# Two neighbouring chunks per block transpose of Q and K, the odd chunks moved to their partitions by transfers

## The chip, the core and the metric

One core of one Trainium2 chip runs the whole program. The metric is the device time of one execution in microseconds (us). Before the change three runs took 794.63, 798.83 and 799.25 us, so the median is 798.83 us. The profiled execution of the same kernel took 792.66 us, of which 790.9 us lie between its first and its last instruction (its span); 1.8 us lie around it.

## What is computed

Sixteen sequences of 256 tokens with 256 features go through four blocks, each added to its input and normalised: a Fourier mixing layer with a cumulative sum, a layer of eight gated low-rank experts, softmax attention with 16 heads of 16 features, and a feed-forward layer with ternary weights. The change touches only the attention:

```python
qkv = jnp.einsum('bld,ed->ble', x, W_qkv)
qkv = qkv.reshape(b, 3, H, L, D_H)              # H = 16, L = 256, D_H = 16
Q, K, V = (qkv[:, 0], qkv[:, 1], qkv[:, 2])
scores = jnp.einsum('bhqd,bhkd->bhqk', Q, K) * D_H ** (-0.5)
attn = jax.nn.softmax(scores, axis=-1)
out = jnp.einsum('bhqk,bhkd->bhqd', attn, V)
out = out.transpose(0, 2, 1, 3).reshape(b, L, D_IN)
return jnp.einsum('bld,ed->ble', out, W_o)
```

Two things in it matter here. The reshape doesn't split the features into heads: the 256 x 768 numbers of one sequence are read on as one row, cut into chunks of 16, and 256 chunks in a row are one head of Q, K or V. One token holds 48 chunks (`NJ`), so a head takes the chunks of 5 1/3 tokens. And softmax does not care in which order the keys are summed, so long as keys and values agree, nor does a row of the result depend on where its query stands.

## The kernel before

**Groups and stages.** The sequences go in four groups of four (`GB = 4`). `attention(i)` handles group i: a projection stage, a first pass over the scores for the row maxima, a second pass for exp and the product with V, and the output projection. `front(b)` computes the first two blocks of a sequence, `back(b)` the feed-forward block. While `attention(i)` runs, the fronts of group i+1 and the backs of group i-1 are worked in between. The projection stage of a group begins only after the last score of the group before it has been read, because it writes over the same tile `zt`; so the four attentions stand one behind the other.

**Projection and transposes.** The 256 tokens of each sequence are cut into 8 blocks `tb` of 32 tokens. For each block TensorE makes a tile of 128 partitions (4 sequences x 32 tokens) by 768 in two PSUM banks (L831, 64 instructions in a group: 32 chunks in one bank, 16 in the other). For the six blocks that hold Q and K VectorE transposes blocks of 32 x 32 from PSUM into `zt` (L840). A chunk has 16 features and the block wants 32, so each chunk is read twice: partitions 32g to 32g+15 of `zt` hold the features of sequence g, partitions 32g+16 to 32g+31 a second copy that nothing uses, except that partition 32g+16 is overwritten later. Blocks 5 to 7 (part of K, and V) are also copied to SBUF (`evacuate`) and sent to HBM (`vd`, L849), from where V is read back with one key in each partition (L868).

**The extra row.** Partition 32g+16 is a seventeenth feature: ones for the keys (L858), and for the queries the negative row maximum (L914). With it, one matmul gives score minus maximum. In the first pass (L894) the scores of one head are taken for all four sequences (16 instructions), VectorE reduces each bank to row maxima (L903, four for a head), and after four heads TensorE transposes the maxima (L907), ScalarE copies them to `nmT` (L908) and transfers put them into their rows of `zt` (L914). The second pass (L933) reads them; then follow exp on ScalarE (L942), the product with V (L948), a transpose back by VectorE (L956) and the division by the sum.

**Queues.** Every transfer is issued from SyncE's queue (SP), in one order. The transfers go round eight semaphores, and each waits until the transfer eight places before it has landed.

**The order of work.** The kernel records its operations first. A planner (`Order.run`) then takes, at each step, the operation that could start earliest by its own table of durations, ties broken by `order.prio`, and pins that order on every engine. Each engine's order is therefore fixed before the run, whatever the true durations are. The order of heads is 14, 15, 0, 1, 2, 3, 4, 5, 12, 13, 6 ... 11, that of the blocks 5, 2, 0, 3, 6, 7, 1, 4.

The places that the prediction names:

| line before | what |
|---|---|
| L831, L840 | projection matmuls; block transposes into `zt` |
| L849, L868 | V out to HBM; V back |
| L858, L914 | row of ones for the keys; negative maxima for the queries |
| L894, L903 | first-pass scores; their maxima |
| L933, L942, L948, L956 | second-pass scores; exp; product with V; transpose back |
| L977, L981, L991 | attention output: transposes, their copy into `oT`, output projection |
| L1027, L1056 | feed-forward matmuls of a back |

Of the kernel before, what the change touches and what calls it, by code (L numbers as in the profile page):

```python
# [18 lines left out]
P = 128  # L19
D = 256  # L20
S = 256
# [264 lines left out]
def forward(ctx, tc, x, xt, wq, wkv, wo0T, f0, degen, cs, wqkvT, wo1T, wfc, wproj, cst, out):  # L286
# [23 lines left out]
    ztv = zt_.rearrange("p (l j) -> p j l", j=NJ)  # L310
# [508 lines left out]
    def attention(i):  # L819
# [4 lines left out]
        for n, tb in enumerate((5, 2, 0, 3, 6, 7, 1, 4)):  # L824
            order.prio = base - 60.0 + n
            for j0, nj in ((0, 32), (32, 16)):
# [10 lines left out]
                if tb < ZT:  # L837
                    dve(
                        [(z[tb], j0)], [b], nj * 32,
                        lambda b=b, tb=tb, j0=j0, nj=nj: V.transpose(  # L840
                            ztv[:, j0 : j0 + nj, ts(tb, 32)], b.v.unsqueeze(2).to_broadcast([P, nj, 2, HD])
                        ),
                        us=nj * 32 * 1.72e-3,
                    )
                if tb >= VT // 32:
# [7 lines left out]
                    )  # L853

            heads = [h for h in range(H) if k_at(h) == tb]
            for g in range(GB if heads else 0):
                op(
                    (SP, 0.1, lambda g=g, lo=ZQ + heads[0] * S, n=len(heads) * 2: nc.sync.dma_start(  # L858
                        zt_[32 * g + HD : 32 * g + HD + 1, lo : lo + n * P].rearrange("o (c q) -> o c q", q=P),
                        a(ones)[0:1, :].unsqueeze(1).to_broadcast([1, n, P]),  # L860
                    )),
                    [(rowk[tb], g)], [ones, z[tb]],
                )
        order.prio = base - 20.0
        for half, lo, n, at in ((0, 28, 4, 12), (0, 0, 12, 0), (1, 12, 16, 0)):
            for g in range(GB):
                op(
                    (SP, 0.5, lambda g=g, half=half, lo=lo, n=n, at=at: nc.sync.dma_start(  # L868
                        va[half][:, at : at + n, g, 0:HD],
                        vd.slot.ap[g].rearrange("t e -> (t e)")[(2 * ZQ + lo * P) * HD - VT * NJ * HD :][: n * P * HD].rearrange("(n p d) -> p n d", p=P, d=HD),  # L870
                    )),
                    [(v[half], (g, at))], [vd],
                )

        def part(g, rows, which, h, at=0, n=S):
            lo = which * ZQ + h * S + at
            return zt_[32 * g : 32 * g + rows, lo : lo + n]
# [7 lines left out]
        for q in range(4):  # L885
            nm, nmT, heads = tile_("nm", [P, GB, 4, 2]), tile_("nmT", [32, P]), HEADS[4 * q : 4 * q + 4]
            for k, h in enumerate(heads):
                order.prio = base + 6.0 * (4 * q + k - 8)
                sc = [ps([P, 2, S], "a") for _ in range(GB)]

                def go(sc=sc, h=h):
                    for t in range(2):
                        for g in range(GB):
                            T.matmul(  # L894
                                sc[g].v[:, t, :], part(g, HD, 0, h, t * P, P), part(g, HD, 1, h),
# [4 lines left out]
                for g in range(GB):  # L900
                    dve(
                        [(nm, (k, g))], [sc[g]], 512,
                        lambda nm=nm, sc=sc, g=g, k=k: V.tensor_reduce(nm.v[:, g, k, :], sc[g].v, AX.X, ALU.max, negate=True),  # L903
# [3 lines left out]
            pe([b], [nm, small], 0.11, lambda b=b, nm=nm: T.transpose(b.v, nm.v.rearrange("p g h t -> p (g h t)"), ident))  # L907
            act([nmT], [b], 128, lambda b=b, nmT=nmT: A.copy(nmT.v, b.v))  # L908
            runs = [heads] if heads[3] - heads[0] == 3 else [heads[0:2], heads[2:4]]
            for g in range(GB):  # L910
                for r, run in enumerate(runs):
                    n = len(run) * 2
                    op(
                        (SP, 0.1, lambda g=g, lo=run[0] * S, n=n, at=8 * g + r * n, nmT=nmT: nc.sync.dma_start(  # L914
                            zt_[32 * g + HD : 32 * g + HD + 1, lo : lo + n * P].rearrange("o (c q) -> o c q", q=P),
                            nmT.v[at : at + n, :],
                        )),
                        [(rowq[q], (g, r))], [nmT, *{q_at(h): z[q_at(h)] for h in run}.values()],
                    )

        for hp in range(H // 2):
            av = ps([P, 2, S], "a")
            for hk in range(2):
                n = hp * 2 + hk
                h = HEADS[n]
                order.prio = base + 6.0 * n
# [227 lines left out]
```

## Time and profile before

Engine time in the profiled execution (792.66 us, span 790.9 us, mean granted TensorE clock 0.921):

| engine | busy us | share of the span |
|---|---|---|
| TensorE matmuls (PE) | 744.1 | 94% |
| TensorE weight loads (PEld, beside PE) | 527.2 | 67% |
| VectorE (DVE) | 642.3 | 81% |
| ScalarE (ACT) | 476.6 | 60% |
| GpSimd (POOL) | 124.0 | 16% |

The four projection stages start at 100.05, 238.45, 421.46 and 589.85 us, and the first second-pass score of each group (L933) at 152.59, 291.43, 477.20 and 642.43 us. Before 100 us the fronts of the first group run, after 722 us only the backs of the last one.

Transfers issued from SP for the attention, in the whole program:

| line | what | count | KB each |
|---|---|---|---|
| L849 | V out | 24 | 256 or 128 |
| L858 | ones | 64 | 2 or 6 |
| L868 | V back | 48 | 32, 96 or 128 |
| L914 | maxima | 96 | 2 or 4 |

A row of groups reads: line, engine, operation, output from input, shapes, count; after the bar busy us and mean ns of one; after the second bar the idle time of the engine just ahead, and who ended it. In the timeline a row merges neighbouring instructions of one line: start, us, engine, line, operation, names, count, and in brackets the idle time ahead. "PE busy" counts a matmul until its modelled end, so that a TensorE that waits in small steps or runs at a lower clock still looks busy. SP's transfers are listed with the time the queue spends on issuing.

### The profile page before, as it was taken

What the parts mean: (1) busy time and instruction counts of PE and PEld (TensorE: products, weight loads), DVE (VectorE), ACT (ScalarE), POOL (GpSimd) and SP (SyncE); (2) the same over time, 40 slices, a digit from 0 to 9 for tenths busy, and PEclk for the clock granted to TensorE, in tenths of its full rate; (3) what the DMA queues carried; (4) which work ended last, traced back from release to release, by engine and by line L of the source; (5) the groups of instructions that cost most, each with busy time, mean ns of one, the idle gap of its engine ahead of it and who ended that gap; (6) DMA issues with size and microseconds to landing.
All of it is one profiled execution on the core that took longest, in us unless ns stands there. A gap on an engine that the chain in (4) does not pass through costs nothing.

```text
span 790.9 us, 15263 instructions
## 1 busy us (share of the span) xinstructions
PE 744.1 (94%) x5664; PEld 527.2 (67%) x5664; DVE 642.3 (81%) x1513; ACT 476.6 (60%) x942; POOL 124.0 (16%) x306
## 2 busy tenths in 40 slices
PE   9999499999999999999999999999989999999794
PEld 6786256665566667777676767765566787766784
DVE  1999989888987997998789999897567978756554
ACT  5865531238782238988765644966721297875973
POOL 1022000101110020222122012021020002011123
PEclk9999699679999988999999989997989699999986
DMA  8101015200001450001011350000001700000000
GB/s 292 40 27 41 13 24 79 57 15 16 29 15 25 67 69 2 16 27 30 2 40 49 60 38 16 15 16 2 15 1 35 76 10 16 14 16 15 1 28 27
DMA packets 87662, 27.18 MB, mean 34 GB/s; under 512 B 68700, under 2 KB 84900, under 8 KB 87588
## 3 DMA queue, kind: packets, MB, share of 16 engines
q1 hardware_dynamic: 87588, 26.21, 15.7%
q8 instruction: 45, 0.74, 0.4%
q14 instruction: 29, 0.24, 0.1%
HBM read 16.76 MB, written 8.91 MB: 32 GB/s over the span
## 4 chain that ended last, share of the span: by engine, by line
PE 68%; DVE 18%; ACT 9%; issue 3%; POOL 2%; DVEq 0%; ACTq 0%; POOLq 0%
PE bank L831 10%; PE bank L894 9%; PE bank L948 8%; PE bank L933 8%; PE bank L1056 7%; PE bank L609 5%; DVE nm L903 5%; PE bank L1027 5%; PE bank L991 3%; PE bank L708 3%; PE bank L793 2%; PE bank L732 2%; DVE st L569 2%; ACT zt L942 1%; ACT hi L1044 1%
## 5 line engine op out<-in xcount | busy, mean ns | idle before, releaser
L942 ACT ACTIVATE zt<-bank 128x512 f32<-128x512 f32 x256 | 133.4, 596 | 57.2 <-PE bank L933 52.3
L903 DVE TENSOR_REDUCE nm<-bank 128x2 f32<-128x512 f32 x256 | 158.8, 679 | 11.1 <-PE bank L894 10.2
L563 POOL TENSOR_SCALAR st<-st 128x2 f32<-128x2 f32 x80 | 23.4, 293 | 535.6 <-DVE st L571 369.7
L894 PE MATMUL bank<-zt 16*128 16x256 f32 x1024 | 100.4, 445 | 2.2 <-DVE nm L903 1.7
L894 PEld LDWEIGHTS bank<-zt 16*128 16x128 f32 x1024 | 63.7, 205 | 29.9 <-DVE nm L903 8.7
L831 PE MATMUL bank<-wqr,x2T 128*128 128x512 f32 (+1 forms) x256 | 83.2, 486 | 0.0
L933 PE MATMUL bank<-zt 17*128 17x256 f32 x1024 | 82.5, 415 | 0.3 <-DVE nm L903 0.3
L948 PE MATMUL bank<-zt,v 128*32 128x256 f32 x1024 | 78.6, 412 | 0.0
L1027 PE MATMUL bank<-xs,w1T 128*128 128x256 f32 x512 | 75.3, 299 | 0.5 <-DVE xs L1017 0.4
L1056 PE MATMUL bank<-w2T,hi 128*128 128x256 f32 x256 | 72.1, 312 | 3.5 <-ACT hi L1044 2.5
L1056 PE MATMUL bank<-w2T,lo 128*128 128x256 f32 x256 | 69.1, 302 | 6.0 <-DVE lo L1046 6.0
L1027 PEld LDWEIGHTS bank<-xs,w1T 128*128 128x128 f32 x512 | 67.6, 199 | 9.2 <-issue 3.7
L840 DVE STREAM_TRANSPOSE zt<-bank 128x1024 f32<-128x1024 f32 (+1 forms) x48 | 64.2, 1456 | 11.3 <-PE bank L831 5.0
L831 PEld LDWEIGHTS bank<-wqr,x2T 128*128 128x128 f32 x256 | 48.5, 190 | 34.2 <-issue 28.5
L933 PEld LDWEIGHTS bank<-zt 17*128 17x128 f32 x1024 | 51.8, 191 | 22.5 <-issue 12.4
L609 PE MATMUL bank<-wf,x 128*128 128x512 f32 x128 | 62.8, 623 | 0.0
L1056 PEld LDWEIGHTS bank<-w2T,hi 128*128 128x128 f32 x256 | 52.8, 206 | 14.1 <-issue 9.1
L564 POOL TENSOR_TENSOR st<-st,mhalf 128x2 f32<-128x2 f32 x80 | 59.4, 743 | 6.8 <-POOL st L563 0.2
L1056 PEld LDWEIGHTS bank<-w2T,lo 128*128 128x128 f32 x256 | 52.7, 206 | 7.5 <-DVE lo L1046 7.5
L1046 DVE TENSOR_TENSOR lo<-work,hi 128x512 fp32r<-128x512 f32 x64 | 42.7, 681 | 15.9 <-ACT hi L1044 15.8
L948 PEld LDWEIGHTS bank<-zt,v 128*32 128x32 f32 x1024 | 29.7, 114 | 35.1 <-issue 14.8
L1036 ACT ACTIVATE work<-bank 128x512 f32<-128x512 f32 x64 | 37.8, 591 | 20.4 <-PE bank L1027 16.2
(196 smaller groups left out, 1260.2 us busy)
## 6 DMA issues: line engine op xcount, KB each, us to landing
x<-in_xT SPq DMA_DIRECT2D x16, 256.0 KB
out<-work SPq DMA_DIRECT2D x16, 256.0 KB
x<-in_x SPq DMA_DIRECT2D x12, 256.0 KB
vd<-work SPq DMA_DIRECT2D x12, 256.0 KB
v<-vd SPq DMA_DIRECT2D x16, 128.0 KB
vd<-work SPq DMA_DIRECT2D x12, 128.0 KB
v<-vd SPq DMA_DIRECT2D x16, 96.0 KB
oT<-in_wfc SPq DMA_DIRECT2D x4, 256.0 KB
```

Of the source, the lines that this page charges most:

```text
L564: pool([dst], [dst, mhalf], 0.7, lambda: G.tensor_tensor(dst.v, dst.v, a(mhalf)[:, 0:n], ALU.pow))
L609: T.matmul(pb.v.rearrange("p a s k -> p (a s k)"), xT.v[:, c, ts(t, P)], a(wf)[:, c].rearrange("p a s f -> p (a s f)"), start=(c == 0), st ...
L831: T.matmul(b.v.rearrange("p j d -> p (j d)"), x2T.v[:, c, tb].rearrange("p g k -> p (g k)"), a(wqr)[:, c, j0 * HD : (j0 + nj) * HD], start ...
L840: lambda b=b, tb=tb, j0=j0, nj=nj: V.transpose(ztv[:, j0 : j0 + nj, ts(tb, 32)], b.v.unsqueeze(2).to_broadcast([P, nj, 2, HD])),
L894: T.matmul(sc[g].v[:, t, :], part(g, HD, 0, h, t * P, P), part(g, HD, 1, h), start=True, stop=True,)
L903: lambda nm=nm, sc=sc, g=g, k=k: V.tensor_reduce(nm.v[:, g, k, :], sc[g].v, AX.X, ALU.max, negate=True),
L933: T.matmul(sc[g].v[:, c, :], part(g, HD + 1, 1, h, c * P, P), part(g, HD + 1, 0, h), start=True, stop=True,)
L942: act([e], [sc[g]], 512, lambda e=e, sc=sc, g=g: A.activation(e.v, sc[g].v, AF.Exp, scale=HD ** -0.5))
L948: T.matmul(av.v[32 * g : 32 * g + 32, hk, :], v_part(g, h, c), es[g].v[:, c, :], start=(c == 0), stop=(c == 1),)
L1027: T.matmul(pb.v[:, i, :], a(w1T)[:, n // 2, ts(q * 2 + i, P)], xs.v[:, n % 2, n // 2, :], start=(n == 0), stop=(n == 3),)
L1046: dve([(lo, q)], [h, (hi, q)], 512, lambda h=h, part=part: V.tensor_tensor(part(lo), h.v, part(hi).bitcast(F32), ALU.subtract), us=0.63)
L1056: T.matmul(pw.v[:, t, :], part.v[:, k, ts(t, P)], a(w2T)[:, k, :], start=(k + n == 0), stop=(k + n == HID // P),)
```

## The change

The 32 x 32 block is now filled by two neighbouring chunks instead of one chunk twice. A transpose thus reads each chunk once and writes half as many elements: even chunks land in partitions 32g to 32g+15 as before, odd chunks in 32g+16 to 32g+31. The odd ones must lie in the first 16 partitions for the matmul, so for each block and sequence a transfer moves them there, into a second half of `zt` that starts at column `ODD` = 4608. Queries and keys of a head now stand in two halves, 128 even and 128 odd; the same holds for the maxima and for V, which is read back in two transfers, even and odd keys. On the way out, the copy into `oT` puts even and odd queries back in turn. The rows of ones and of maxima are written once for each half, so their transfers double in number and halve in size. The matmuls keep their count and sizes; a moving operand is now two stretches of 128 columns. The planner gets a shorter duration for the transpose; the rewritten priorities have the same values as before.

```diff
-    ztv = zt_.rearrange("p (l j) -> p j l", j=NJ)
+    ODD = ZT * 32 * NJ // 2
+    ztv = zt_[:, 0:ODD].rearrange("p (l j) -> p j l", j=NJ // 2)
+    zt2 = zt_[:, 0 : 2 * ODD].rearrange("p (t c) -> p t c", t=2)
...
                     dve(
-                        [(z[tb], j0)], [b], nj * 32,
+                        [(z[tb], j0)], [b], nj * HD,
                         lambda b=b, tb=tb, j0=j0, nj=nj: V.transpose(
-                            ztv[:, j0 : j0 + nj, ts(tb, 32)], b.v.unsqueeze(2).to_broadcast([P, nj, 2, HD])
+                            ztv[:, j0 // 2 : (j0 + nj) // 2, ts(tb, 32)],
+                            b.v.rearrange("p (j t) d -> p j (t d)", t=2),
                         ),
-                        us=nj * 32 * 1.72e-3,
+                        us=nj * HD * 1.43e-3,
                     )
...
+            if tb < ZT:
+                width = 32 * NJ // 2
+                for g in range(GB):
+                    op(
+                        (SP, 0.1, lambda g=g, lo=tb * width: nc.sync.dma_start(
+                            zt_[32 * g : 32 * g + HD, ODD + lo : ODD + lo + width],
+                            zt_[32 * g + HD : 32 * g + 2 * HD, lo : lo + width],
+                        )),
+                        [(z[tb], ("odd", g))], [(z[tb], 0), (z[tb], 32)],
+                    )
...
             for g in range(GB if heads else 0):
-                op(
-                    (SP, 0.1, lambda g=g, lo=ZQ + heads[0] * S, n=len(heads) * 2: nc.sync.dma_start(
+                for t in range(2):
+                    op(
+                        (SP, 0.1, lambda g=g, lo=t * ODD + (H + heads[0]) * P, n=len(heads): nc.sync.dma_start(
...
-                        [(rowk[tb], g)], [ones, z[tb]],
+                        [(rowk[tb], (g, t))], [ones, z[tb]],
...
-                    (SP, 0.5, lambda g=g, half=half, lo=lo, n=n, at=at: nc.sync.dma_start(
-                        va[half][:, at : at + n, g, 0:HD],
+                for t in range(2):
+                        (SP, 0.3, lambda g=g, t=t, half=half, lo=lo, n=n, at=at: nc.sync.dma_start(
+                            va[half][:, at + t : at + n : 2, g, 0:HD],
...
-        def part(g, rows, which, h, at=0, n=S):
-            lo = which * ZQ + h * S + at
-            return zt_[32 * g : 32 * g + rows, lo : lo + n]
+        def some(g, rows, which, h, t):
+            lo = t * ODD + (which * H + h) * P
+            return zt_[32 * g : 32 * g + rows, lo : lo + P]
+        def every(g, rows, which, h):
+            lo = (which * H + h) * P
+            return zt2[32 * g : 32 * g + rows, :, lo : lo + P]
...
-                                sc[g].v[:, t, :], part(g, HD, 0, h, t * P, P), part(g, HD, 1, h),
+                                sc[g].v[:, t, :].rearrange("p (t q) -> p t q", t=2), some(g, HD, 0, h, t), every(g, HD, 1, h),
...
-                        (SP, 0.1, lambda g=g, lo=run[0] * S, n=n, at=8 * g + r * n, nmT=nmT: nc.sync.dma_start(
+                    for t in range(2):
+                            (SP, 0.1, lambda g=g, t=t, lo=t * ODD + run[0] * P, n=len(run), at=8 * g + 4 * t + r * 2, nmT=nmT: nc.sync.dma_start(
...
-        oT = tile_("oT", [P, 2, GB, S // 32, 32])
+        oT = tile_("oT", [P, 2, GB, P, 2])
...
-                    lambda c=c, half=half: oT.v[:, c, :, half * 4 : half * 4 + 4, :].rearrange("p g u k -> p u g k"),
+                    lambda c=c, half=half: oT.v[:, c, :, :, half].rearrange("p g (u k) -> p u g k", k=32),
```

## The prediction

> **What bounds the kernel now.** I read the page first: how busy the engines are, and which engines the chain of work that ended last runs through.
>
> ```profile
> PE 744.1 (94%) x5664; PEld 527.2 (67%) x5664; DVE 642.3 (81%) x1513; ACT 476.6 (60%) x942; POOL 124.0 (16%) x306
> PE 68%; DVE 18%; ACT 9%; issue 3%; POOL 2%; DVEq 0%; ACTq 0%; POOLq 0%
> ```
>
> TensorE leads, VectorE comes second, so halving a VectorE operation could pay. Where it pays depends on the stage, so next I cut the first two attentions at the start of the projection, at its end and at the first second-pass score. Columns: busy us of PE, PEld, DVE, ACT, POOL, then clock, DMA share, GB/s.
>
> ```profile
> 100.00:120.80 20.80, 20.80 (x68) 11.99 (x66) 17.77 (x20) 7.03 (x12) 0.00 (x0) 1.00 0.12 29
> 120.80:152.60 31.80, 31.37 (x218) 23.43 (x219) 29.33 (x56) 5.82 (x14) 1.71 (x5) 0.79 0.49 72
> 152.60:238.40 85.80, 83.08 (x774) 50.63 (x768) 74.96 (x210) 59.18 (x128) 12.16 (x35) 0.92 0.06 20
> 238.40:259.20 20.80, 20.80 (x66) 12.05 (x65) 16.38 (x17) 3.45 (x9) 0.00 (x0) 1.00 0.12 29
> 259.20:291.40 32.20, 32.20 (x247) 20.97 (x246) 31.25 (x68) 8.40 (x17) 3.73 (x11) 0.99 0.55 79
> 291.40:421.50 130.10, 129.62 (x1140) 95.86 (x1140) 114.22 (x307) 106.26 (x209) 30.54 (x80) 0.95 0.07 20
> ```
>
> Three stages, three limits. The projection is PE's: its 64 matmuls stand in the chain as one piece of 20.6 us without a gap. From there to the first second-pass score VectorE is nearly full (29.3 of 31.8 us), with the maxima L903. After that PE is full again. The transposes lie in the first stage, where VectorE is not what ends it. Third, SP's queue in the second attention:
>
> ```profile
> 254.91 3.15 SPq L849 DMA_DIRECT2D vd<-work  x4
> 266.56 6.50 SPq L868 DMA_DIRECT2D v<-vd  x8
> 273.16 3.57 SPq L858 DMA_DIRECT2D zt<-ones  x4
> 276.83 4.08 SPq L868 DMA_DIRECT2D v<-vd  x4
> 281.00 1.46 SPq L351 DMA_DIRECT2D x<-in_x  x1
> 282.56 0.42 SPq L351 DMA_DIRECT2D x<-in_xT  x1
> 283.07 5.03 SPq L914 DMA_DIRECT2D zt<-nmT  x8
> ```
>
> The maxima of the first four heads had been copied to nmT at 276.22, but SP reaches them at 283.07 and is through at 288.1. The first second-pass score starts at 291.43. In the other attentions SP is through 2.9, 9.2 and 2.8 us before it. So SP's queue is 3 us from being the path in three attentions of four, and the change adds to this queue.
>
> **The transposes.**
>
> ```profile
> L840 DVE STREAM_TRANSPOSE zt<-bank 128x1024 f32<-128x1024 f32 x24 | 45.3, 1890 | 9.9 <-PE bank L831 5.0 <-DMA zt<-ones 2.9 <-ACT work L369 2.0
> L840 DVE STREAM_TRANSPOSE zt<-bank 128x512 f32<-128x512 f32 x24 | 24.5, 1022 | 1.4 <-ACT work L369 1.4
> L956 DVE STREAM_TRANSPOSE work<-bank 128x512 f32<-128x512 f32 x32 | 22.8, 712 | 24.6 <-PE bank L948 24.4
> ```
>
> Now 69.8 us. The new forms are 512 and 256 elements. Nearest row: 512 of L840 takes 1.022; its slope is (1.890 - 1.022) / 512 = 1.695 ns, so 256 takes 1.022 - 0.434 = 0.588. That is 24 x 1.61 = 38.6 us. Lower bound: L956, which writes without a stride, 0.712, and half of it for 256: 24 x 1.068 = 25.6. I take 38.6 (same operation, also strided): 31.2 us of VectorE time less, 7.8 in each attention; up to 44.2 by the other end.
>
> The Trainium skill (Vector Engine (DVE) Microarchitecture Reference, the part on the reshape block) says a transpose sustains one element per cycle per lane, and VectorE: DVE Perf Modes (Specifications) gives 0.96 GHz. Worked out from these, an estimate, 768 elements fewer per block would save 0.80 us instead of the 1.30 by the rows, or 19 us in all; the measured slope decides.
>
> What of the 31.2 us is on the path? PE runs through the projection in any case. Exposed is the end: the last transposes end at 122.7, and the first maxima start there, 1.9 us after the first scores; elsewhere L903 follows its scores by 1.2. So 0.7 to 1.9 us in an attention; I take 1, 4 in all. The rest lets later VectorE work come earlier only where TensorE has fed it. After the first second-pass score PE is idle 2.7, 0.5, 8.2 and 1.8 us of its stages; half of this 13 I credit to a freer VectorE: 6 us. Bounds of both together: 0 and 31 (44).
>
> **The transfers.** Per attention the change adds 24 odd moves, 16 for ones, 12 for V, 24 for maxima: 58 become 134. I walk SP's queue from its first vd to the last of the first maxima, in the order of the built program, by the spacing of its rows in the trace: 0.62 for a 2 or 4 KB row transfer (start to start), 0.76 for 12 pieces, 0.65 between them for 6, 0.66 to 0.8 for vd, 0.5 for V in 4-row pieces and 0.9 for 12 rows, of which I take 0.6 for 6. An odd move (16 rows of 3 KB) has no row; I bound it by 0.41 (an x load) and 0.76 and take 0.62, nmT's, also within SBUF. Sum: vd 2 x 0.66 = 1.3; odd 8, 5.0; ones 16, 9.9; odd 8, 5.0; vd 4, 3.15; odd 1, 0.6; ones 8, 5.2; odd 7, 4.3; V 5, 2.5; ones 8, 5.2; V 3, 1.5; V 8, 4.8; maxima 16, 9.9. To this comes what is left of SP's wait for vd to land (8.4 us, 257.9 to 266.5; now 5.8 of it is filled): 2.6. Together 61 us. Before the same stretch was 241.0 to 288.1, 47.1 us. Bounds for the 24 odd moves alone: 16 of them lie ahead of vd, so the stretch is 56 to 64.
>
> From the first vd (102.6, 241.0, 426.3, 594.3) that puts the end of SP's maxima at 163.6, 302.0, 487.3 and 655.3. The last maxima of before landed 1.05 us after issue, so the second pass can start at 164.6, 303.1, 488.3 and 656.4 instead of 152.6, 291.4, 477.2, 642.4: 12.0, 11.7, 11.1 and 14.0 later, 48.8 us in all. Who waits: L933 on PE, and behind it, PE's order being fixed, everything queued there, then exp, and VectorE's L956. The planner counts 0.43 us for each issue and knows part of it: by the built order and PE's chain pieces (1.08 for a head's scores, 1.15 for eight L1027 or L1056, 1.73 for eight L991), the work between projection and first L933 goes from 22.5, 28.7, 29.4, 21.8 us to 19.6, 37.8, 39.2, 29.5. So 23.7 us net are brought forward: 48.8 - 23.7 = 25.1 us lost. If nothing brought forward counts, 49.
>
> The Trainium skill (DMA: Bandwidth & Descriptors, Rules for kernel authors) speaks against this change: many small transfers should be put together into one large one. The section on issuing engines there calls the issue time small relative to the transfer. Here the row says 0.62 us of issue against 1.05 to land, and with 16 in a row the issue is what counts; by the page's rule alone the doubling would cost one transfer's latency, about 1 us an attention.
>
> **At nothing.** The odd halves of the first heads: their moves end near 263.6, the third head's scores came at 267.1. Scores with two stretches of 128 columns: same count and columns; nothing covers them, and each per cent on the 183 us of L894 and L933 would be 1.8 us; I take none. The strided copy into oT: 16 copies of 0.59 on ACT, beside PE's 1.9 us transposes; doubled, 9 us of ACT, little of it on the path. V back: the same 64-byte packets.
>
> **Sum.** 25.1 - 4 - 6 = +15 us: 792.66 becomes 807.7. The median of the runs is 6.2 us above the profiled one, so I predict 798.8 + 15 = 814.
>
> **Rivals.** (a) Faster: VectorE's freed 31 to 44 us are on the path. For it: 18% of the chain is DVE, and PE's 94% hides small waits. Against it: where the transposes run, PE stands in one piece. It decides if the stretch before L933 shrinks by more than SP's delay, which needs SP through by 150 in the first attention, not 163. Then 7.8 x 4 less: 768 (755 at the lower bound). (b) No change: the planner's brought-forward work fills the wait in all but the first attention, so that only its 12.0 + 2.9 us remain, less the 10 credited: 804. (c) The delay counts in full and PE's clock falls after each wait, as at 290 to 304: 798.8 + 49 - 4 = 844. (d) The transpose isn't shorter, the write being what it pays for: then the 10 credited go and it is 824.
>
> **Numbers.** My forecast (with d) 0.53, (c) 0.10, (b) 0.17, (a) 0.20. Its own range is 806 to 836. The range of all must leave out no more than 0.2: 788 to 840. A measurement of this kernel tells about 1% from no change (790.8 to 806.8): slower 0.63, same 0.17, faster 0.20.
>
> **What would show it.** L840 at 1.0 and 0.6 us; SP busy without a gap from the first vd to the maxima, ending some 61 us later; first L933 62 to 66 us after the projection starts instead of 53 to 56; PE waiting there for a transfer; a longer time at more idle PE. I am wrong if the first L933 comes by 55 us, or if it comes late and PE has caught up by the next projection.

## The result: 862 us, 8% slower

The changed kernel takes 861.71 us (median of 4 runs, 859.53 to 863.09) beside 798.81 for the kernel before on the same chip: a ratio of 1.080, 95% interval [1.075, 1.084]. The forecast was 814, its range ended at 840. The profiled execution took 862.93, with a span of 861.2 instead of 790.9. The ratios below leave out executions that ran slower at a lower granted clock, the medians do not, and three experiments (e6, e8, e12) were profiled in such an execution, so no lags are taken from their traces.

The page of the changed kernel, its busy times and its chain of work by engine:

```profile
PE 780.7 (91%) x5664; PEld 543.6 (63%) x5664; DVE 625.2 (73%) x1510; ACT 479.6 (56%) x945; POOL 122.2 (14%) x306
...
PE 59%; DVE 17%; ACT 10%; SPq 6%; issue 4%; DMA 2%; POOL 2%; DVEq 0%; ACTq 0%; POOLq 0%
```

PE has the same 5664 matmuls and fell from 94% of the span to 91%; VectorE, at 73% instead of 81%, has become freer. New in the chain is SP's queue with 6% and a DMA with 2%. The page gives 36.6 us more of PE's busy time and 33.7 more of idle time; how much of the first goes with the granted clock, whose mean went from 0.921 to 0.890, was not told apart.

The second attention in stages, cut at the start of the projection, at its end and at the first second-pass score (length; busy us of PE, PEld, DVE, ACT, POOL; then clock, DMA share, GB/s):

```profile
269.80:290.50 20.70, 20.70 (x66) 11.95 (x64) 16.67 (x37) 5.68 (x11) 0.40 (x1) 1.00 0.19 39
290.50:333.90 43.40, 41.60 (x313) 33.42 (x312) 40.55 (x87) 19.55 (x37) 8.55 (x26) 0.92 0.29 50
333.90:441.40 107.50, 104.03 (x925) 70.88 (x924) 88.64 (x236) 82.92 (x168) 19.04 (x50) 0.95 0.16 37
```

The projection takes as long as before. The middle stage, from the end of the projection to the first second-pass score, has grown from 32.2 to 43.4 us, and VectorE is busy in it with 87 instructions instead of 68, since work from later was brought in. What ended the stage is in SP's queue in the same attention (start, us, transfer):

```profile
275.63 6.82 SPq L863 DMA_DIRECT2D zt<-zt  x8
282.50 9.63 SPq L874 DMA_DIRECT2D zt<-ones  x16
292.23 5.79 SPq L863 DMA_DIRECT2D zt<-zt  x8
298.11 3.20 SPq L854 DMA_DIRECT2D vd<-work  x4
...
303.15 8.42 SPq L874 DMA_DIRECT2D zt<-ones  x8
311.61 4.37 SPq L863 DMA_DIRECT2D zt<-zt  x7
316.02 2.67 SPq L885 DMA_DIRECT2D v<-vd  x5
318.73 5.67 SPq L874 DMA_DIRECT2D zt<-ones  x8
324.45 5.50 SPq L885 DMA_DIRECT2D v<-vd  x10
330.05 9.71 SPq L936 DMA_DIRECT2D zt<-nmT  x16
```

There is hardly a gap in it. The maxima, which left SP at 283.07 to 288.1 before, now leave from 330.05 to 339.8: 60.3 us after the start of the projection instead of 44.6. Each of these transfers takes some 0.6 us of issue, the moves of 48 KB (median 0.59) as the ones (0.65) and the maxima (0.56) of a few KB. PE's waits say who pays (us in total, times, longest; L955 are second-pass scores, L916 first-pass scores, L999 the transposes of the attention's output):

```profile
PE bank L955 <- DMA zt<-nmT: 23.4, 12, 5.3
...
PE bank L916 <- ACT work L653: 6.1, 1, 6.1
...
PE bank L999 <- ACT work L653: 2.9, 1, 2.9
```

The first line is the second-pass scores waiting for their maxima, 23.4 us; in the kernel before no such wait is listed. How this looks in PE's timeline, in the first attention (start, us, then in brackets the idle time ahead):

```profile
163.47 1.19 PE L955 MATMUL bank<-zt 17*128 17x256 f32 x2 [4.68 <-DMA zt<-nmT]
165.89 1.19 PE L955 MATMUL bank<-zt 17*128 17x256 f32 x2 [1.24 <-DMA zt<-nmT]
168.30 1.19 PE L955 MATMUL bank<-zt 17*128 17x256 f32 x2 [1.23 <-DMA zt<-nmT]
170.72 2.04 PE L955 MATMUL bank<-zt 17*128 17x256 f32 x10 [1.23 <-DMA zt<-nmT]
```

Two matmuls, a wait of 1.2 us, two matmuls, a wait: PE advances at SP's pace, 2.42 us from step to step, which is the time SP takes for the four transfers of one group (4 x 0.6). The other two lines of the waits, 9.0 us together, are not in the prediction. They go back to a copy on ScalarE, whose own waits (us in total, times, longest) say for what it stood:

```profile
ACT work L653 <- DMA vd<-work: 15.3, 2, 9.8
```

L653 needs a `work` tile. The writes of V to its DRAM buffer `vd` hold such tiles until they have landed, and four of them now stand behind 16 moves and 16 ones in SP's queue: at 298.11 above, 28.3 us after the start of the projection; before, at 254.91, it was 16.5. A late transfer thus also holds back a copy, and PE behind it.

The lag of the second pass sums the loss up. Its second head (in PE's order) came 57.3, 65.1, 68.7 and 61.2 us after the start of its projection; now 79.5, 82.1, 86.7 and 78.8. That is 74.7 us more in the four attentions. From there to the next projection or to the end the four take 433.9 us instead of 438.5. So the whole loss (70.3 us of span) lies ahead of the second head of the second pass.

### The profile page after: what moved, and what is told of

It reads as the page before. It is cut to its first block, busy times and chain, and to the rows that moved or that the text cites. A ratio compares the mean times of both kernels' runs of the same rounds, so it can differ in the third digit from the quotient of the medians.

```text
span 861.2 us, 15650 instructions
## 1 busy us (share of the span) xinstructions
PE 780.7 (91%) x5664; PEld 543.6 (63%) x5664; DVE 625.2 (73%) x1510; ACT 479.6 (56%) x945; POOL 122.2 (14%) x306
## 3 DMA queue, kind: packets, MB, share of 16 engines
q1 hardware_dynamic: 91428, 30.93, 16.9%
## 4 chain that ended last, share of the span: by engine, by line
PE 59%; DVE 17%; ACT 10%; SPq 6%; issue 4%; DMA 2%; POOL 2%; DVEq 0%; ACTq 0%; POOLq 0%
PE bank L834 10%; PE bank L955 8%; PE bank L970 8%; PE bank L1078 7%; PE bank L916 6%; PE bank L612 4%; PE bank L1049 3%; SPq L936 3%; DVE nm L925 3%; PE bank L711 3%; ACT work L1061 2%; DVE st L572 2%; PE bank L1013 2%; ACT work L1067 2%; PE bank L558 2%
## 5 line engine op out<-in xcount | busy, mean ns | idle before, releaser
L925 DVE TENSOR_REDUCE nm<-bank 128x2 f32<-128x512 f32 x256 | 159.4, 684 | 36.9 <-PE bank L916 34.5
L955 PE MATMUL bank<-zt 17*128 17x256 f32 x1024 | 108.9, 469 | 26.2 <-DMA zt<-nmT 23.4
L916 PE MATMUL bank<-zt 16*128 16x256 f32 x1024 | 99.6, 430 | 7.9 <-ACT work L653 6.1
L955 PEld LDWEIGHTS bank<-zt 17*128 17x128 f32 x1024 | 64.7, 216 | 61.9 <-issue 40.4
L970 PE MATMUL bank<-zt,v 128*32 128x256 f32 x1024 | 84.6, 442 | 0.0
L916 PEld LDWEIGHTS bank<-zt 16*128 16x128 f32 x1024 | 62.6, 196 | 33.9 <-issue 8.3
L1078 PE MATMUL bank<-w2T,hi 128*128 128x256 f32 x256 | 79.4, 335 | 4.0 <-ACT hi L1066 2.6
L1078 PE MATMUL bank<-w2T,lo 128*128 128x256 f32 x256 | 75.7, 322 | 6.4 <-DVE lo L1068 6.4
L1049 PE MATMUL bank<-xs,w1T 128*128 128x256 f32 x512 | 71.9, 294 | 2.2 <-DVE nm L925 0.8
L834 PEld LDWEIGHTS bank<-wqr,x2T 128*128 128x128 f32 x256 | 48.8, 192 | 36.4 <-issue 30.9
L844 DVE STREAM_TRANSPOSE zt<-bank 128x512 f32<-128x512 f32 (+1 forms) x48 | 50.4, 1145 | 25.2 <-PE bank L834 21.1
L1078 PEld LDWEIGHTS bank<-w2T,hi 128*128 128x128 f32 x256 | 58.4, 228 | 14.8 <-issue 8.9
L1078 PEld LDWEIGHTS bank<-w2T,lo 128*128 128x128 f32 x256 | 58.5, 228 | 7.9 <-DVE lo L1068 7.8
L970 PEld LDWEIGHTS bank<-zt,v 128*32 128x32 f32 x1024 | 31.5, 120 | 44.2 <-issue 27.2
L978 DVE STREAM_TRANSPOSE work<-bank 128x512 f32<-128x512 f32 x32 | 22.8, 712 | 47.0 <-PE bank L970 40.8
```

Of the source, the lines that this page charges most:

```text
L834: T.matmul(b.v.rearrange("p j d -> p (j d)"), x2T.v[:, c, tb].rearrange("p g k -> p (g k)"), a(wqr)[:, c, j0 * HD : (j0 + nj) * HD], start ...
L844: lambda b=b, tb=tb, j0=j0, nj=nj: V.transpose(ztv[:, j0 // 2 : (j0 + nj) // 2, ts(tb, 32)], b.v.rearrange("p (j t) d -> p j (t d)", t=2),),
L916: T.matmul(sc[g].v[:, t, :].rearrange("p (t q) -> p t q", t=2), some(g, HD, 0, h, t), every(g, HD, 1, h), start=True, stop=True,)
L925: lambda nm=nm, sc=sc, g=g, k=k: V.tensor_reduce(nm.v[:, g, :, k], sc[g].v, AX.X, ALU.max, negate=True),
L955: T.matmul(sc[g].v[:, c, :].rearrange("p (t q) -> p t q", t=2), some(g, HD + 1, 1, h, c), every(g, HD + 1, 0, h), start=True, stop=True,)
L970: T.matmul(av.v[32 * g : 32 * g + 32, hk, :], v_part(g, h, c), es[g].v[:, c, :], start=(c == 0), stop=(c == 1),)
```

## The experiments

Theory 1: SP's queue. The extra transfers make the first maxima late. Theory 2: the layout, that is slower transposes, operands in two stretches, strided copies. Theory 3: the planner, which counts 0.43 us for an issue where the trace has 0.6, made an order in which the second pass comes too early for its maxima. The table gives, as means over the four attentions of the profiled execution, the transfers on SP between the start of the projection and the first maxima, the lag of the first of these maxima, and the lag of the second head of the second pass.

| run | edit | ahead | first maxima | second head | median us | ratio to before, 95% |
|---|---|---|---|---|---|---|
| before | | 35 | 43.8 | 63.1 | 798.8 | 1 |
| after | | 78 | 60.8 | 81.7 | 861.7 | 1.080 [1.075, 1.084] |
| e1 | no moves | 54 | 44.9 | 68.0 | 817.7 | 1.024 [1.019, 1.030] |
| e2 | ones together | 54 | 46.3 | 68.7 | 814.1 | 1.022 [1.017, 1.028] |
| e3 | both | 30 | 36.6 | 66.9 | 808.3 | 1.015 [1.007, 1.022] |
| e4 | before, transfers split | 63 | 55.7 | 75.0 | 843.6 | 1.059 [1.054, 1.064] |
| e5 | ones together, new plan | 62.5 | 54.9 | 75.1 | 839.6 | 1.054 [1.047, 1.061] |
| e6 | e5, moves from GpSimd | 38.5 | - | - | 826.0 | 1.034 [1.028, 1.039] |
| e7 | before, ones together | 23 | 39.4 | 63.5 | 797.4 | 1.000 [0.997, 1.003] |
| e8 | e3, contiguous transposes | 30 | - | - | 808.0 | 1.009 [1.005, 1.013] |
| e9 | order of before | 87 | 72.4 | 92.3 | 917.5 | 1.151 [1.146, 1.156] |
| e10 | e3 in order of before | 39 | 42.1 | 64.7 | 801.5 | 1.005 [1.001, 1.010] |
| e11 | e9, ones together, moves from GpSimd | 39 | 49.9 | 70.8 | 837.2 | 1.052 [1.046, 1.058] |
| e12 | 0.60 us an issue | 58 | - | - | 820.7 | 1.022 [1.015, 1.030] |
| e13 | ones together, 0.60 | 57 | 48.1 | 68.9 | 817.1 | 1.022 [1.016, 1.027] |
| e14 | before, 0.60 | 35 | 44.2 | 64.0 | 796.4 | 0.997 [0.995, 1.000] |
| e15 | V behind the maxima | 62.5 | 51.7 | 73.5 | 839.8 | 1.050 [1.044, 1.057] |
| e16 | e13 with V behind | 36 | 36.9 | 67.4 | 807.8 | 1.007 [1.002, 1.012] |
| e17 | vd from GpSimd | 72 | 56.0 | 75.8 | 841.8 | 1.055 [1.051, 1.059] |

**e1 to e4: is it the queue?** In e1 to e3 the planner's order stays: the transfers are taken out, or put together, after it has been made. In e4 each transfer of the kernel before is issued as two.

```diff
 # e1: the moves are planned, and not issued
-    lambda g=g, lo=tb * width: nc.sync.dma_start(
+    lambda g=g, lo=tb * width: None and nc.sync.dma_start(
 # e2: one transfer for the four groups, at the first one's place; e3 is e1 and e2
-    lambda g=g, ...: nc.sync.dma_start(
-        zt_[32 * g + HD : 32 * g + HD + 1, lo : lo + n * P] ...
-        a(ones)[0:1, :] ...
+    lambda g=g, ...: g == 0 and nc.sync.dma_start(
+        zt_[HD : 3 * 32 + HD + 1 : 32, lo : lo + n * P] ...
+        a(ones)[0:4, :] ...
 # e4, in the kernel before, and likewise for V and the maxima
+    [nc.sync.dma_start(..., lo + t * n * P : lo + (t + 1) * n * P ...) for t in range(2)]
```

> The changed kernel with its 96 moves of odd chunks (24 in each attention) left out of SyncE's queue, and every other instruction in the same order on every engine; the odd half of the columns then holds stale values, so the scores of odd chunks are not the reference's. Theory 1 (SyncE issues its transfers one after another, about 0.6 us each, and the first maxima stand at the end of that walk): 24 x 0.63 = 15 us come off the walk ahead of the first maxima of each attention; the first scores of the second pass start some 53 to 57 us after the projection's start instead of 61 to 66, and 30 to 60 of the 63 us lost come back: 800 to 830 us. Theory 2 (the layout: slower transposes, operands in two stretches): the moves have no part in it, 850 to 862 us. Theory 3 (the planner put second-pass scores where they must wait for any walk): the order is the same, so a gain here speaks for it no more than for theory 1.

> The changed kernel with the rows of ones written for the four groups by one transfer with four destination partitions instead of four transfers with one each: 32 become 8 in each attention, everything is computed as before, and the order on every engine is the same otherwise. Theory 1: 24 x 0.6 = 14 us come off SyncE's walk in each attention, as in the run without the moves: 800 to 835 us, first scores of the second pass at 53 to 58 us after the projection's start. Theory 2: 856 to 864 us.

> The changed kernel with the moves of odd chunks left out (stale odd halves, so other scores than the reference's) and the ones of four groups in one transfer: 48 issues fewer in each attention, same order otherwise. Theory 1: SyncE's walk is shorter than in the kernel before (86 against 58 transfers, but most of the difference lies behind the first maxima), and what is left over the kernel before is layout and clock: 785 to 812 us; the gain over each of the two single edits is much less than their sum, since the walk stops being what ends last. Theory 2: 848 to 862 us.

> The kernel before, with each transfer of ones, of V and of maxima split into two of half the size (58 become 110 in each attention), same order on every engine, same layout, same transposes, no moves of odd chunks. Theory 1: 16 more ones and 12 more V ahead of the first maxima are 28 x 0.6 = 17 us, of which a few are slack: 10 to 15 us in each attention, 835 to 865 us. Theory 2: transfers alone cost little, 797 to 808 us.

All four times fall where theory 1 has them. The first second-pass scores of e1 and e2 do not: expected at 53 to 58 us, they came at 49 to 64. In the second attention they came at 64 us in e1, e2 and e3 alike, as in the changed kernel (64.1), though the maxima left there 13 to 24 us earlier; what sets them there is the planned order on PE, which these three edits keep. e1 and e2 take away 24 issues of quite different transfers, and get back 44 and 48 us of the 63; both together get back 53, much less than the sum, since the queue then no longer ends last. e4 has neither the layout nor the moves, and loses 47 us by transfers alone. SP's rows in the second attention of e2 (four ones, two ones, 16 maxima):

```profile
272.38 2.91 SPq L874 DMA_DIRECT2D zt<-ones  x4
...
297.51 1.25 SPq L874 DMA_DIRECT2D zt<-ones  x2
...
305.89 9.73 SPq L936 DMA_DIRECT2D zt<-nmT  x16
```

A transfer into four partitions takes SP no longer (median 0.59 us for the 32 ones of e2) than one into a single partition (0.65 for the 128 of the changed kernel). In e4 PE now waits for maxima in the kernel before:

```profile
PE bank L933 <- DMA zt<-nmT: 8.7, 8, 1.3
```

**e5 to e8: a new plan, another queue, another write.**

```diff
 # e5: 8 operations instead of 32, so the planner knows of it; e7 the same in the kernel before
-            for g in range(GB if heads else 0):
+            for g in range(0, GB if heads else 0, 4):
 # e6: e5 and
-    (SP, 0.1, lambda g=g, lo=tb * width: nc.sync.dma_start(
+    (POOL, 1.0, lambda g=g, lo=tb * width: nc.gpsimd.dma_start(
 # e8: e3 and
-    ztv[:, j0 // 2 : (j0 + nj) // 2, ts(tb, 32)],
+    zt_[:, tb * 32 * NJ // 2 + j0 * 16 : tb * 32 * NJ // 2 + (j0 + nj) * 16].rearrange("p (j l) -> p j l", l=32),
```

> The changed kernel with the ones of the four groups in one transfer, as in the run e2, but planned anew: the planner now knows of 24 transfers fewer in each attention and may put the second pass earlier. Theory 1 alone: what e2 left over the kernel before (about 17 us) is a fixed order that still keeps the second pass for later; with a new order 800 to 814 us, the second attention's first second-pass score at 54 to 60 us after the projection's start instead of 63.6. Theory 3 (the planner counts 0.43 us per issue where the trace has 0.6, so its new order again comes too early for the transfers): 812 to 835 us, with PE waiting over 8 us for the maxima's transfers. Theory 2: as e2, 811 to 818.

> The changed kernel with the ones of the four groups in one transfer and the moves of odd chunks issued by GpSimd instead of SyncE, planned anew; everything is computed. Theory 1: SyncE is left with 86 issues in each attention and the first maxima leave about as early as in the kernel before: 790 to 808 us. GpSimd issues 24 transfers in each attention at up to 1 us (no row shows its price); its own work is 122 us of the span, so it has room, and only a late odd half ahead of the first scores would show, as a wait of the first scores on a move. Theory 2: 845 to 862.

> The kernel before with the ones of the four groups in one transfer (16 become 4 in each attention), planned anew; everything is computed. In the trace of before TensorE waits for no transfer of maxima ahead of its second-pass scores, so by theory 1 SyncE's walk ended first there and 12 issues fewer (7 us) are worth nothing by themselves: 792 to 802 us. If the walk bounds the kernel before as well, 5 to 7 us in each attention come off: 770 to 780 us.

> The run e3 (no moves of odd chunks, ones of four groups together, same order on every engine) with the block transposes writing their blocks one beside the other instead of interleaved with a stride of 24 elements; the queries and keys are then permuted and the scores not the reference's, while every other instruction has the same shape. Theory 2, now for what e3 left over the kernel before (about 12 us): transposes of 512 elements fall from 1.45 to about 0.71 us and of 256 from 0.84 to about 0.4 us, 55 us in all to about 28; if VectorE ends the path from the projection to the first scores, 2 to 4 us in each attention come back: 792 to 802 us. If the order on TensorE is what is left: 803 to 810 us, no change.

e5 surprised, above the ranges of all three theories: the same transfers as e2, and 25 us slower. The planner had 24 issues to spare in its own account and put all of V ahead of the maxima (SP's queue in the second attention of e5, then PE's wait):

```profile
308.15 9.81 SPq L885 DMA_DIRECT2D v<-vd  x16
318.05 9.72 SPq L936 DMA_DIRECT2D zt<-nmT  x16
```

```profile
PE bank L955 <- DMA zt<-nmT: 16.0, 8, 6.1
```

So the number of transfers is not what counts, but how many stand ahead of the first maxima: 62.5 here, 54 in e2. e6 missed its range of 790 to 808 as well; the planner had again put all of V ahead, and e11 below shows a second cause. e7 is the control for the kernel before: 12 issues fewer change nothing there, since PE waits for no maxima in it. In e8 the transposes, writing without interleaving, take half:

```profile
L844 DVE STREAM_TRANSPOSE zt<-bank 128x512 f32<-128x512 f32 x24 | 17.2, 715 | 39.6 <-PE bank L834 37.1 <-ACT work L372 2.3
...
L844 DVE STREAM_TRANSPOSE zt<-bank 128x256 f32<-128x256 f32 x24 | 10.7, 445 | 3.4 <-ACT work L372 0.9
```

That is 27 us of VectorE time less than the 55.0 us below, and no gain can be told from the noise: the ratio is 1.009 [1.005, 1.013] beside e3's 1.015 [1.007, 1.022]. Most of what the transposes take is not on the path there; a gain of some us, up to about 1%, is not excluded.

**e9 to e12: the order.** For e9 to e11 the planner is left out, and a recorded order is issued: that of the kernel before on every engine, the halves of split transfers one behind the other, the moves behind their transposes.

```diff
-            lo = min(found, key=lambda f: f[0])
...
-            at, o, w, cost = min(others, key=lambda f: f[0] + f[3])
+            n, way, spots = plan[done]
+            o, w = ops[n], ops[n].ways[way]
 # e10: with the edits of e3; e11: with e2's and the moves on GpSimd
 # e12, planned:
-ISSUE = 0.43
+ISSUE = 0.6
```

> All of the changed kernel's work (134 transfers in each attention, everything computed), but issued in the order in which the kernel before has it on every engine, the second halves of split transfers right behind the first and the moves of odd chunks behind their transposes. Theory 3 (the planner's new order is what lost the time): close to the kernel before, 797 to 815 us. Theory 1: some 24 moves, 16 ones and 12 V transfers more stand ahead of the first maxima, 52 x 0.6 = 31 us, and the order of before puts less other work in front of the second pass to cover them: 25 to 30 us in each attention, 880 to 915 us, worse than the changed kernel.

> The changed layout (transposes of pairs, scores in two stretches, strided last copies) in the order of the kernel before, with the moves of odd chunks left out (stale odd halves, so other scores than the reference's) and the ones of four groups in one transfer: ahead of the first maxima stand about as many transfers as in the kernel before (12 more of V, 8 fewer of ones). This prices the layout alone. Theory 1: the layout costs nothing; with 15 us of VectorE saved in transposes and little of it on the path, 788 to 802 us. Theory 2: over 806 us.

> Everything computed, in the order of the kernel before on TensorE, VectorE and ScalarE, the ones of four groups in one transfer and the moves of odd chunks issued by GpSimd, so that SyncE's walk is about as long as before. Theory 1: 790 to 808 us, near the run with the layout alone and better than the run e6 by 15 us or more, since e6 had the planner's order with all of V ahead of the maxima. If the moves land late from GpSimd's queue, first-pass scores wait for them: 810 to 830 us.

> The changed kernel, everything computed, planned anew with 0.60 us for each issue on SyncE in place of 0.43, which is what the trace shows. Theory 3 (a wrong price made the order): the planner puts other work where TensorE waited 23 us for the maxima's transfers and the held work tiles 9 us: 820 to 840 us. Theory 1: the walk is as long as before and the second pass starts as late, only the wait is filled with work that is then missing later: 850 to 865 us.

e9 is the dearest of all, 2.5 us over theory 1's range: 87 transfers ahead, and an order with nothing to cover them. So the planner's new order had already saved 56 us; as "order lost the time" theory 3 falls. PE's waits (here L1105 are second-pass, L1066 first-pass scores):

```profile
PE bank L1105 <- DMA zt<-nmT: 39.3, 16, 11.4
PE bank L1066 <- ACT work L1208: 14.8, 1, 14.8
PE bank L1066 <- DMA zt<-zt: 14.3, 2, 12.4
```

e10 prices the layout: 801.5 us, half a per cent over the kernel before [0.1, 1.0]. Its stage ahead of the first second-pass score in the second attention is that of before again, 32.5 us with 30.97 of VectorE:

```profile
265.40:297.90 32.50, 32.50 (x249) 21.01 (x247) 30.97 (x69) 8.50 (x17) 3.77 (x11) 0.99 0.43 61
```

So theory 2 accounts for some 4 of the 63 us, at most 8 by the interval. e11 missed by being too slow: the moves left SP, but SP's ones follow them into the same blocks, and SP stood still for them (SP's waits):

```profile
SPq L1024 <- DMA zt<-zt: 36.4, 15, 7.6
```

e12 keeps all 134 transfers and gets back some 46 us, by the planner's price alone (the ratio falls from 1.080 to 1.022; by the medians it is 41). The median lies in theory 3's range and not in theory 1's, 850 to 865, which took the walk ahead of the maxima to stay as long. SP's queue in its second attention shows how:

```profile
298.06 5.77 SPq L874 DMA_DIRECT2D zt<-ones  x8
303.93 9.70 SPq L936 DMA_DIRECT2D zt<-nmT  x16
313.68 11.41 SPq L885 DMA_DIRECT2D v<-vd  x18
```

V now goes behind the first maxima (18 transfers at 313.68), so that 58 transfers stand ahead of them on average instead of 78. With the true price the planner put less ahead of what is urgent here.

**e13 to e17: price, place of V, and `vd`.**

```diff
 # e13: e5 with ISSUE = 0.6; e14: the kernel before with ISSUE = 0.6
 # e15: V's transfers created after the first four heads, and for the planner dependent on their maxima
-                        [(v[half], (g, at, t))], [vd],
+                        [(v[half], (g, at, t))], [vd, rowq[0]],
 # e16: e13 and e15 together
 # e17, planned as before:
-                        (SP, 0.1, lambda st=st, tb=tb, j0=j0, nj=nj: nc.sync.dma_start(
+                        (SP, 0.1, lambda st=st, tb=tb, j0=j0, nj=nj: nc.gpsimd.dma_start(
```

> The changed kernel, everything computed, with the ones of four groups in one transfer, planned with 0.60 us for each issue instead of 0.43. Run e5 (same transfers, 0.43) took 840 us with 62 transfers ahead of the first maxima, all of V among them. Theory 1 (what counts is how late the first maxima leave, whoever sets it): the planned queue still has 20 of V's 24 transfers ahead of them, 58 in all, so only a little better, 820 to 838 us. Theory 3 (the true price by itself lets the planner fill the wait): 798 to 815 us.

> The kernel before, unchanged but planned with 0.60 us for each issue instead of 0.43. A control: if the true price gains here as much as in the changed kernel (41 us in e12), the price has nothing to do with the loss. Theories 1 and 3: with 58 transfers TensorE waits for no maxima in the kernel before, and the price decides nothing: 790 to 805 us. Against both: 755 to 775 us.

> The changed kernel with all its 134 transfers and the old price of 0.43 us, everything computed, but V's transfers planned behind the first maxima: 13 to 20 of them stood ahead of those in each attention. Theory 1: 16 x 0.6 = 9 us off the walk ahead of the first maxima, which leave 50 to 53 us after the projection's start: 818 to 838 us, about as the run e12 in which the planner itself had put most of V behind them. If V now comes late, e times V waits for it and the gain is lost: 850 to 865 us. Theory 2: 858 to 864 us.

> The changed kernel, everything computed, with three edits to the queue and the plan together: the ones of four groups in one transfer, V's transfers planned behind the first maxima, 0.60 us for each issue. 38 transfers stand ahead of the first maxima, about as many as the 34 in the kernel before. Theory 1: the loss is gone but for the layout's half per cent: 793 to 808 us. Theory 2: over 840 us. A gain on the kernel before, under 790 us, would show that the layout has something to give once the queue is out of the way.

> The changed kernel, everything computed, with only the six writes of V to its DRAM buffer in each attention issued by GpSimd instead of SyncE, every other instruction in the same order. In the changed kernel they stand behind moves and ones in SyncE's queue, hold work tiles, and the trace shows TensorE waiting 6.1 + 2.9 us behind copies that waited for those tiles. Theory 1: those 9 us go, and six issues fewer on SyncE bring the first maxima 6 x 0.6 = 3.6 us earlier in each attention, of which most counts since TensorE waits for them: 840 to 854 us. If the held tiles cost nothing beside the late maxima: 848 to 856. If GpSimd's issues are late or slow: 860 or more.

e14 is the control: in the kernel before the price is worth nothing that can be told from no change. It matters only where the queue is what is late. e13 against e5: the true price is worth 22 us, and lands between the two theories' ranges. e15 came out 2 us over its range, and its waits show the part that V's place does not touch: the held tiles are still there (L904 are first-pass, L956 second-pass scores, L1000 the transposes of the attention's output).

```profile
PE bank L904 <- ACT work L653: 6.0, 1, 6.0
...
PE bank L956 <- DMA zt<-nmT: 4.0, 3, 1.8
...
PE bank L1000 <- ACT work L653: 2.9, 1, 2.9
```

e17 takes that away, with the order of everything kept: no wait for L653 is left, and it gains 20 us. But six issues fewer stand ahead of the first maxima too, and they leave 4.8 us earlier in each attention (56.0 instead of 60.8). So how much of the 20 us the held tiles cost is not shown; PE's own waits behind them were 9.0. The wait for the maxima is still there:

```profile
PE bank L955 <- DMA zt<-nmT: 19.1, 8, 9.2
```

e16 puts three edits together. 36 transfers stand ahead of the maxima; these leave 36.9 us after the projection's start, and V follows them (second attention):

```profile
282.55 9.72 SPq L924 DMA_DIRECT2D zt<-nmT  x16
292.31 15.23 SPq L937 DMA_DIRECT2D v<-vd  x24
```

That is 807.8 us, 0.7% over the kernel before, with everything computed and 110 transfers in each attention. No version of the changed kernel beat the kernel before.

The column of the second head orders the runs: 4 times its growth over before, added to 797, is within 10 us of the median of every row that has it. (Heads are counted within each attention; in e16 the third projection begins before the second attention's last head.) The lag of the first maxima does not order them: in e3 and e16 they leave 7 us earlier than before, PE waits for none of their transfers, and the second head is still 4 us later. e10, with the edits of e3 in the order of before, has it at 64.7 and takes 801.5 us. So what e3 still loses goes, for the most part, with the planner's new order on PE; for e16 this was not tried.

## Why the prediction was wrong

**Right.** The prediction had SP's queue as what ends last, its walk with hardly a gap, PE waiting for the maxima's transfers, and the time of the first second-pass score: 63.1, 64.1, 66.1 and 61.0 us after the projection's start (foretold 62 to 66). The sign and this part of the mechanism stand, by e1 to e4.

**The step that failed** is "So 23.7 us net are brought forward: 48.8 - 23.7 = 25.1 us lost". Both of its terms were off.

The delay was taken up to the *first* second-pass score (foretold 48.8, measured 40.5 in all). But that is not where the waiting ends. The walk up to the last of the first maxima is 65.4 us in the second attention, 66.5 on average, not 61 (in the second attention the 24 moves take 18.9 us of it, their waits included, not 14.9), and PE goes through the scores two by two while they land. To it comes a wait that the prediction did not have: it counted `vd` into the walk, but did not ask who waits for `vd`. PE's waits behind it are 9.0 us. Up to the second head the delay is 74.7 us: 40.5 up to the first, and 34.2 from the first to the second. e3 has the same order on PE and waits for no maxima; that stretch in the second attention of the changed kernel, then of e3 (columns as above):

```profile
333.91:351.84 17.93, 14.56 (x90) 10.30 (x89) 8.80 (x20) 9.25 (x18) 1.59 (x5) 0.71 0.41 49
311.46:320.21 8.75, 8.57 (x89) 6.81 (x89) 8.73 (x20) 8.62 (x18) 2.35 (x5) 1.00 0.09 29
```

The same work takes twice as long, with PE idle for part of it and the granted clock at 0.71 instead of 1.00. Over the four attentions it is 72.7 us, in e3 36.3, before 38.5.

The 23.7 us brought forward were credited in full, and at most 4.6 us came back (433.9 instead of 438.5 behind the second head). e3 shows it without the wait: there the first second-pass scores come 17.4 us later than before, summed over the attentions, because other work stands ahead of them, and the time behind the second head is 437.8 us, only 0.7 shorter. What the planner brought forward was work of other sequences; the first pass of the attention itself stands behind the waiting scores in PE's fixed order. Its tenth head, in both kernels between the first two heads of the second pass, came at 76 to 79 us after the projection's start instead of 54 to 63. That the attention's own work queued behind the wait is why so little came back is argued, not shown.

**The credits** of 4 and 6 us for faster transposes were wrong too: e8 takes another 27 us off VectorE and gains nothing that can be told, and e10, the layout alone, is 0.5% slower, not 10 us faster. The transposes themselves were mis-sized, and outside the stated bounds:

```profile
L844 DVE STREAM_TRANSPOSE zt<-bank 128x512 f32<-128x512 f32 x24 | 34.9, 1453 | 24.3 <-PE bank L834 21.1 <-ACT work L372 2.6 <-issue 0.5
...
L844 DVE STREAM_TRANSPOSE zt<-bank 128x256 f32<-128x256 f32 x24 | 20.1, 836 | 0.9 <-ACT work L372 0.9
```

1.453 and 0.836 us instead of 1.022 and 0.588, so 55.0 us in all: 14.8 saved, not 31.2. By e8 it made little difference here.

**The rivals.** (a), faster, is refuted by e8 and e10. (b), the wait filled in all attentions but the first, fails: the second heads come 17.0 to 22.2 us later in all four. (d), transposes no shorter, is half right (1.453 us for what took 1.890) and, at 824, still 38 us short. (c), the delay in full and a falling clock, comes nearest, at 844 and with a chance of 0.10; it also lacked `vd` and the walk's last 5 us. Its example does not show its rule, though: the granted clock from 291.4 to 303.5 us is 0.50 in the kernel before, but PE is listed as busy without a gap from 259.2 to 291.4. "At nothing": the odd moves of the first heads did land in time (PE's waits list none for `zt` from `zt` in the changed kernel; e9 has two, 14.3 us together), and the rest of that list is within e10's half a per cent.

**The planner's part.** Of the 63 us, some 46 would not have been lost with the true price of an issue (e12), and nothing of the kind was to be had before (e14). Both readings hold together: the transfers make the maxima late, and the planner's price hides from it that they are late. The shares do not add up, as e1 to e3 show. How much of the loss is the granted clock alone was not tried.

## What to carry to other kernels

A transfer costs its issue on the queue, here some 0.6 us for a few KB as for 48, and what a longer queue costs is read from the most urgent transfer at its end: count what stands ahead of it. Follow a delay to the last of the transfers that a stage needs and to every buffer that a late transfer holds, and credit work "brought forward" only as far as what comes later gets shorter: here 4.6 of 23.7 us did. A planner's constants are part of the kernel: when a change moves the bound to another queue, check its price against the trace first.

## What the runs showed of the hardware

- A block transpose that writes interleaved (stride of 24 elements) takes 1453 and 836 ns for 512 and 256 elements, a slope of 2.41 ns an element; written contiguously (e8) 715 and 445, a slope of 1.05. Before, with a stride of 48 and each chunk read twice, the slope was 1.70. Why the shorter stride is dearer was not tried. The Trainium skill (Vector Engine (DVE) Microarchitecture Reference, the part on the reshape block) has one element per cycle per lane; with the 0.96 GHz of VectorE: DVE Perf Modes (Specifications) that would be an estimated 1.04 ns, which the contiguous form meets and the interleaved one does not.
- SP's issue takes 0.56 to 0.65 us (medians: maxima 0.56, moves of 16 rows of 3 KB 0.59, ones 0.65 in the changed kernel; ones into four partitions 0.59 in e2), so putting four into one saves about three quarters. It does not grow with the size: the loads of `x` of 256 KB took 0.37 to 0.39. The Trainium skill (DMA: Bandwidth & Descriptors, Rules for kernel authors) asks for small transfers to be put together; here it pays by the issue.
- GpSimd issued the moves at 0.49 us each (47.0 us for 96 in e11) and the writes to `vd` at 0.71 (16.9 for 24 in e17), about SP's price; the moves landed 4.4 us after their issue (median, e11).
